# 4-bit FFN in a fused two-layer kernel: gate and up of three token units as three float32r passes over split digits

## Chip, cores and metric

The kernel runs on one core of a Trainium2 chip. Times are device microseconds of one execution; the time of the kernel before is the median of three runs, 622.34 us (621.92 to 623.31). The profile is of one further execution, 623.01 us, of which 620.9 us lie between its first and last instruction. TensorE is called PE (its weight loads PEld), VectorE DVE, ScalarE ACT, GpSimd POOL, and SP issues the DMAs.

## What is computed

Two transformer layers on 2 x 512 tokens of width 256. Each of the four steps has the form x = x + LN(f(LN(x))):

```
x = x + LN(attention(LN(x)))           # 16 heads of 128, rope, causal softmax, wo
x = x + LN(ffn_4bit(LN(x)))            # gate, up: 256 -> 2048, down: 2048 -> 256
x = x + LN(linear_attention(LN(x)))    # qkv, phi(q)*cumsum(k*v) / (phi(q)*cumsum(k)), W_out
x = x + LN(ffn_lut(LN(x)))             # 256 -> 688 -> 256, weights are 16 table values
```

The 4-bit FFN, which the change is about:

```
gate = xt @ Wg.T ; up = xt @ Wu.T      # Wg, Wu [2048, 256]: 4-bit codes times a scale per 32
inter = gelu_tanh(gate) * up
out = inter @ Wd.T                     # Wd [256, 2048]
```

## The kernel before

**Tiling.** The 1024 tokens are four units of 256 (`TU`, L41): units 0 and 1 are batch entry 0, units 2 and 3 entry 1. Attention goes head by head over an entry (32 slots, `slot`, L1149). The rest goes unit by unit. The hidden width 2048 is 16 chunks of 128 rows, `gate` and `up` are the two kinds, and the contraction of 256 is two halves (`NK`).

**PE.** Every product goes through `matmul` (L286), in float32, its 128 weight columns cut into two halves of 64 (`halved`). The profile shows each half as two records. A bank is a PSUM tile of 128 x 512; there are four tags (`mm`, `s`, `t`, `o`) of two banks each (`bank`, L243), so the third user of a tag waits until the first is read.

**4-bit FFN.** `ffn_hidden(u)` (L1089) makes two chunks at a time: four products into a `mm` bank for gate, four into an `s` bank for up, Gelu on ACT from `mm`, and the product `hT` on DVE from `s`. `ffn_out(u)` (L1117) contracts `hT` with the down weights: 32 products into an `o` bank. Its result goes to `after_ffn` (L1134): `norms` (L420) on POOL, DVE and ACT, a 32 x 32 transposition on DVE into `tr` and four DMAs that bring `tr` to `xT` (`brought`, L377), then `linear_attention` (L1340): three projections with `wqkv`, Relu and Exp on ACT, sums on POOL and DVE, running sums (`tensor_tensor_scan`) on DVE, reciprocals, products `lT` on POOL, `wout` on PE, norms again. The running sum of units 1 and 3 starts from the end of units 0 and 2. Last comes the table FFN (`silu_hidden` L1435, `silu_out` L1475).

**What sets the order.** All engines take their instructions in the order in which the program writes them. The program writes PE's work in the order of its loops, and between two pieces of it (`poll`, L262) it lets waiting chains write their next step, when a planner (`Times` L50, `Engine` L103) believes that their inputs are ready. The planner keeps a clock for each engine with a cost for each instruction; for a float32 product PE is charged 5 ns and the streams (L294). All instructions that go through the planner carry its line, L192, and all products L291. `fills` are DVE instructions without a due time, which turn table codes into weights (`select_in`, L451); they are written into gaps that the planner sees on DVE, or all at once by `flush`.

**Order around the change.** Attention of entry 1 ends together with the hidden chunks of unit 0. Then (L1323 to L1325) the attention sums are added on DVE, the remaining fills flushed, and the chain `after_attention(1)` (L1075) begins, which makes the normed and turned tokens `xT1` of units 2 and 3. The main loop (L1537 to L1543) runs, for each unit, the rest of its hidden chunks, the first bank pair of the next unit, and `ffn_out`. So the order on PE is: two banks of unit 1, out of unit 0, the rest of unit 1, two banks of unit 2, out of unit 1, and so on. `xT1` of unit 1 comes from `after_attention(0)`, during attention of entry 1.

Of the kernel before, what the change touches and what calls it, by code (L numbers as in the profile page):

```python
# [10 lines left out]
F32 = mybir.dt.float32  # L11
I32 = mybir.dt.int32
F8 = mybir.dt.float8e4
U8 = mybir.dt.uint8
# [22 lines left out]
TURNED = [P, 4, NK, HT, 32]  # L37
INTER = 688
# [7 lines left out]
AHEAD = 2.4  # L46
REST = INTER - (NO - 1) * P
# [152 lines left out]
def sandwich_kernel(  # L200
# [61 lines left out]
    def poll():  # L262
        while True:
            due = [c for c in chains if c[0] <= now[0]]
            if not due:
                return
            c = min(due, key=lambda c: c[0])
            wait = next(c[1], None)
            if wait is None:
                chains.remove(c)  # L270
            else:
                c[0] = now[0] + wait
# [23 lines left out]

    def transpose(out, in_):
        nc.tensor.transpose(out, in_, ident)  # L298
        now[0] = max(now[0], times.start("PE", [out], [in_])) + 0.11
        times.add("PE", now[0], [out], [in_])  # L300
# [14 lines left out]
    cos_sb = const.tile([P, S], F32, name="cos_sb")  # L315
    sin_sb = const.tile([P, S], F32, name="sin_sb")
    bo_sb = const.tile([P, D], F32, name="bo_sb")
# [59 lines left out]
    def brought(to, tr):  # L377
        for a in range(4):
            sync.dma_start(
                out=to[:, a].rearrange("p k j t -> p (k j t)"),  # L380
                in_=tr[32 * a : 32 * a + 32].rearrange("f c k j t -> f c (k j t)"),
            )

    def last_norms(u, y, to, eps):

        x = [xs[u][:, j, :] for j in range(HT)]

        def factors(y, eps):
            st = small.tile([P, 6], F32, tag="st", name="st")
            mv = small.tile([P, 2], F32, tag="mv", name="mv")  # L390
            vector.bn_stats(st, y)
            vector.bn_aggr(mv, st)
            ve = small.tile([P, 1], F32, tag="ve", name="ve")
            vector.tensor_scalar(ve, mv[:, 1:2], eps, None, ALU.add)
            rstd = small.tile([P, 1], F32, tag="rstd", name="rstd")
            pool.tensor_tensor(rstd, ve, mhalf[:, :1], ALU.pow)
            return mv, rstd

        first = [factors(t, eps) for t in y]
        second = []  # L400
        for j in range(HT):
            add_scaled(x[j], y[j], first[j][1])
            second.append(factors(x[j], EPS))
        yield 1.0
        n = acts.tile([P, HT, D], F32, tag="ln", name=f"n_{u}")
        tr = turning(u, 3)
        for j in range(HT):
            mv, rstd = second[j]
            vector.tensor_scalar(n[:, j, :], x[j], mv[:, 0:1], rstd, ALU.subtract, ALU.mult)
            turned_about(tr, n, j)  # L410
        brought(to, tr)
        yield 1.0
        for j in range(HT):
            mv, rstd = first[j]
            shift = small.tile([P, 1], F32, tag="shift", name="shift")
            pool.tensor_scalar(shift, mv[:, 0:1], rstd, -1.0, ALU.mult, ALU.mult)
            scalar.activation(x[j], x[j], AF.Identity, bias=shift)
        yield until(to)

    def norms(u, y, stage, to, eps=EPS, strided=False):  # L420
# [89 lines left out]
    with ExitStack() as at:  # L510
# [5 lines left out]
        dq = at.enter_context(tc.tile_pool(name="dq", bufs=1))  # L516

# [557 lines left out]
        def after_attention(b):  # L1075
            yield 0.5
            for u in (2 * b, 2 * b + 1):
                xT1[u] = late.get("lw", acts).tile(
                    TURNED, F32, tag="xT1", name=f"xT1_{u}", bufs=2
                )  # L1080

                y = [half(acc, u)[:, j, :] for j in range(HT)]
                yield from norms(u, y, 1, xT1[u], strided=True)
# [3 lines left out]
        hT1 = {}  # L1087

        def ffn_hidden(u):  # L1089
            if u % 2 == 0:  # L1090
                hT1[u] = fh.tile([P, MLP // P, TU], F32, tag="hT", name=f"hT_{u}", bufs=1)
            else:
                hT1[u] = late["lw"].tile([P, MLP // P, TU], F32, tag="hTb", name=f"hT_{u}")
            nc_u = UNIT // P
            for c2 in range(0, MLP // P, 2):
                pg, pu = bank("mm"), bank("s")
                for ps, ws in ((pg, wg_u), (pu, wu_u)):
# [15 lines left out]
                    hT1[u][:, c2 : c2 + 2, :].rearrange("p c t -> p (c t)"), ge, pu  # L1113
# [3 lines left out]
        def ffn_out(u):  # L1117
            po = bank("o")
            for t in range(HT):
                for c in range(MLP // P):  # L1120
# [3 lines left out]
                        hT1[u][:, c, t * P : (t + 1) * P],  # L1124
# [6 lines left out]
            begin(after_ffn(u, po))  # L1131
            yield

        def after_ffn(u, po):  # L1134
            xT2[u] = late["lp"].tile(TURNED, F32, tag="xT2", name=f"xT2_{u}", bufs=1)
            yield from norms(u, [po[:, j * D : (j + 1) * D] for j in range(HT)], 2, xT2[u])
# [12 lines left out]
        def slot(i):  # L1149
# [21 lines left out]
            if i == NH + 2:  # L1171
                attention_sums(0)
                begin(after_attention(0))
# [110 lines left out]
            if i == NS - 4:  # L1284
# [4 lines left out]
                    [(down_i[:, o, :], wd[:, o, :]) for o in range(NO)],  # L1289
# [34 lines left out]
        vector.flush()  # L1324
        begin(after_attention(1))  # L1325


    lw = late["lw"] = ctx.enter_context(tc.tile_pool(name="lw", bufs=1))
    lp = late["lp"] = ctx.enter_context(tc.tile_pool(name="lp", bufs=2))
    gp = ctx.enter_context(tc.tile_pool(name="gp", bufs=2))  # L1330

    ones = lw.tile([P, TU], F32, name="ones")
    pool.memset(ones, 1.0)
    wqkv_sb = lw.tile([P, NK, 3 * D], F32, name="wqkv_sb")
    sync.dma_start(out=wqkv_sb, in_=wqkv)
    wout_sb = lw.tile([P, NK, D], F32, name="wout_sb")
# [3 lines left out]
    def linear_attention(u):  # L1340
# [15 lines left out]

        def of(name, bufs=1):
            return lp.tile([P, NK, TU], F32, tag=name, name=f"{name}_{u}", bufs=bufs)
# [4 lines left out]
        for part, e, f in ((1, ek, k), (0, eq, q)):  # L1363
            ps = project(part, "mm")
            scalar.activation(flat(e), ps, AF.Relu, scale=-1.0)
            scalar.activation(flat(f), ps, AF.Relu)
            if last:

                scalar.activation(e, e, AF.Exp, scale=-1.0)
                vector.tensor_scalar(e, e, -1.0, 1.0, ALU.add, ALU.add)  # L1370
# [3 lines left out]
        ps = project(2, "s")  # L1374
        scalar.copy(flat(v), ps)
        if not last:
# [3 lines left out]
            for e, f in ((ek, k), (eq, q)):  # L1380
                vector.tensor_scalar(e, e, -1.0, 1.0, ALU.add, ALU.add)
                pool.tensor_add(f, f, e)
        yield until(k, v)
        ks, kvs, den, lT = of("ks", 2), of("kvs", 2), of("den"), of("lT")

        def running_sum(to, of_):
            for ch in range(NK):
                before = carry[to is kvs, u - 1][:, ch, TU - 1 :] if u % 2 else 0.0
# [3 lines left out]
            carry[to is kvs, u] = to  # L1392

        running_sum(ks, k)
        if not last:
            yield until(ks, q)
        vector.tensor_mul(den, q, ks)
        vector.tensor_scalar(den, den, EPS_LIN, None, ALU.add)
        vector.tensor_mul(v, k, v)
        yield until(v)  # L1400
        running_sum(kvs, v)
# [23 lines left out]
        yield from last_norms(u, y, t, 16 * EPS) if last else norms(u, y, 3, t, 16 * EPS)  # L1425
# [5 lines left out]
    hT2 = [lw.tile([P, NO, TU], F32, name=f"hT2_{j}") for j in range(2)]  # L1431
    for t in hT2:
        pool.memset(t[:, FULL, :], 0.0)

    def silu_hidden(u):  # L1435
# [12 lines left out]
        for o in range(0, NO, 2):  # L1448
# [11 lines left out]
            si = gp.tile([P, 2 * TU], F32, tag="si", name="si")  # L1460
# [76 lines left out]
    hidden = main  # L1537
    for u in range(NUNIT):
        run(hidden)
        if u + 1 < NUNIT:  # L1540
            hidden = ffn_hidden(u + 1)
            run(hidden, 2)
        run(ffn_out(u))  # L1543
    hidden = None
    vector.flush()
# [102 lines left out]
```

## Time and profile before

| what | value |
|---|---|
| median of three runs | 622.34 us (621.92 to 623.31) |
| profiled execution | 623.01 us, span 620.9 us |
| PE busy | 611.6 us, 99% of the span, 4968 records |
| PEld busy | 389.4 us, 63% |
| DVE busy | 452.0 us, 73%, 1159 instructions |
| ACT busy | 306.2 us, 49%, 716 instructions |
| POOL busy | 226.2 us, 36%, 343 instructions |
| granted PE clock | 1.00 |
| DMA | 75.61 MB, 122 GB/s over the span |

The busy shares are means over the span. Attention and what is beside it lie before 391 us, the 4-bit FFN with most of the linear attention between 391 and 550 us, the table FFN after. A PE record ends, by the profile's model, after the next one has begun, so the step from one start to the next is the time that a record costs. The same holds, to about 0.09 us, for DVE and ACT instructions that don't depend on one another. In the profile's lists a bracket at the end of a line gives the idle time of the engine ahead of the instruction and what ended it.

### The profile page before, as it was taken

What the parts mean: (1) busy time and instruction counts of PE and PEld (TensorE: products, weight loads), DVE (VectorE), ACT (ScalarE), POOL (GpSimd) and SP (SyncE); (2) the same over time, 40 slices, a digit from 0 to 9 for tenths busy, and PEclk for the clock granted to TensorE, in tenths of its full rate; (3) what the DMA queues carried; (4) which work ended last, traced back from release to release, by engine and by line L of the source; (5) the groups of instructions that cost most, each with busy time, mean ns of one, the idle gap of its engine ahead of it and who ended that gap; (6) DMA issues with size and microseconds to landing.
All of it is one profiled execution on the core that took longest, in us unless ns stands there. A gap on an engine that the chain in (4) does not pass through costs nothing.

```text
span 620.9 us, 13496 instructions
## 1 busy us (share of the span) xinstructions
PE 611.6 (99%) x4968; PEld 389.4 (63%) x4968; DVE 452.0 (73%) x1159; ACT 306.2 (49%) x716; POOL 226.2 (36%) x343
## 2 busy tenths in 40 slices
PE   9999999999999999999999999999999999999996
PEld 7555565555556546555555667777777777776665
DVE  7975788988988878877885889972472752472963
ACT  5655666576556476666656662024414223325210
POOL 5344444343243264364444300061161350162531
PEclk9999999999999999999999999999999999999999
DMA  8375867796777767787776423201001000001010
GB/s 230 108 199 147 233 183 204 194 243 179 220 216 204 194 189 199 194 233 200 193 166 156 117 63 73 77 18 35 2 7 30 2 18 18 2 1 35 18 53 18
DMA packets 53393, 75.61 MB, mean 122 GB/s; under 512 B 6992, under 2 KB 34512, under 8 KB 53328
## 3 DMA queue, kind: packets, MB, share of 16 engines
q1 hardware_dynamic: 53328, 74.76, 45.5%
q8 instruction: 39, 0.64, 0.4%
q14 instruction: 26, 0.21, 0.1%
HBM read 28.59 MB, written 1.05 MB: 48 GB/s over the span
## 4 chain that ended last, share of the span: by engine, by line
PE 95%; DMA 2%; DVE 1%; SPq 1%; ACT 0%; issue 0%; POOL 0%; DVEq 0%
PE ps_mm L291 38%; PE ps_o L291 21%; PE ps_s L291 21%; PE ps_t L291 15%; DMA pT<-turned 2%; SPq L174 1%; PE ps_o L556 1%; ACT p L192 0%; DVE rr L192 0%; DVE x L192 0%; DVE centred L192 0%; DVE p L192 0%; ACT ra L192 0%; POOL rstd L192 0%; PE ps_t L298 0%
## 5 line engine op out<-in xcount | busy, mean ns | idle before, releaser
L192 ACT ACTIVATE p<-p,mn 128x512 f32<-128x512 f32 (+3 forms) x128 | 70.4, 551 | 51.9 <-DVE mn L192 51.9
L291 PE MATMUL ps_mm<-xT,wg 128*64 128x256 f32 (+1 forms) x704 | 85.9, 379 | 0.0
L291 PE MATMUL ps_s<-xT,wu 128*64 128x256 f32 x672 | 82.0, 379 | 0.0
L291 PE MATMUL ps_t<-pT,v 128*64 128x256 f32 (+3 forms) x512 | 74.8, 433 | 2.8 <-DMA pT<-turned 2.8
L291 PE MATMUL ps_o<-wd,hT 128*64 128x256 f32 (+1 forms) x704 | 76.7, 375 | 0.0
L291 PEld LDWEIGHTS ps_mm<-xT,wg 128*64 128x64 f32 (+1 forms) x704 | 55.1, 137 | 20.5 <-ACT si L192 0.4
L291 PEld LDWEIGHTS ps_o<-wd,hT 128*64 128x64 f32 x704 | 54.7, 137 | 20.2
L192 DVE TENSOR_TENSOR hT<-ge,ps_s 128x512 f32<-128x512 f32 x32 | 21.8, 684 | 61.2 <-PE ps_s L291 36.9
L291 PEld LDWEIGHTS ps_s<-xT,wu 128*64 128x64 f32 x672 | 52.9, 137 | 19.6 <-DVE hT L192 0.3
L291 PEld LDWEIGHTS ps_t<-pT,v 128*64 128x64 f32 x512 | 39.6, 137 | 40.5 <-issue 32.3
L192 ACT ACTIVATE p<-p,rs 128x512 f32<-128x512 f32 (+3 forms) x128 | 61.1, 550 | 1.8 <-DVE rs L192 1.8
L291 PE MATMUL ps_o<-wo,oT 128*64 128x256 f32 x512 | 61.0, 379 | 0.0
L291 PE MATMUL ps_mm<-xT,wk 128*64 128x512 f32 x248 | 58.8, 592 | 0.9 <-DVE rr L192 0.9
L291 PE MATMUL ps_mm<-xT,wq 128*64 128x512 f32 (+2 forms) x256 | 59.2, 576 | 0.0
L291 PE MATMUL ps_s<-kT,qT 128*64 128x320 f32 (+5 forms) x384 | 57.4, 424 | 0.0
L291 PEld LDWEIGHTS ps_o<-wo,oT 128*64 128x64 f32 x512 | 39.4, 137 | 27.8 <-issue 14.9
L192 DVE STREAM_TRANSPOSE turned<-p 128x512 f32<-128x512 f32 (+3 forms) x128 | 53.8, 476 | 2.9 <-ACT p L192 1.6
L192 POOL TENSOR_TENSOR ra<-ra,cos_sb 128x512 f32<-128x512 f32 (+1 forms) x33 | 41.2, 1249 | 40.5 <-ACT ra L192 40.5
L192 DVE SCALAR_TENSOR_TENSOR ry<-ps_mm,cols_sb,sin_sb 128x512 f32<-128x512 f32 x54 | 40.3, 746 | 21.5 <-ACT ra L192 20.0
L291 PE MATMUL ps_mm<-wv,xTv 128*64 128x256 f32 x464 | 55.3, 379 | 0.0
L192 ACT ACTIVATE ln<-x,shift,rstd 128x256 f32<-128x256 f32 x22 | 13.3, 607 | 77.3 <-POOL shift L192 76.6
L291 PEld LDWEIGHTS ps_s<-kT,qT 128*64 128x64 f32 x384 | 35.9, 137 | 22.4 <-issue 11.6
(162 smaller groups left out, 953.6 us busy)
## 6 DMA issues: line engine op xcount, KB each, us to landing
pT<-turned SPq DMA_DIRECT2D x128, 208.0 KB, 3.9
rr<-ry SPq DMA_DIRECT2D x108, 128.0 KB, 3.0
wo<-in_wo SPq DMA_DIRECT2D x17, 256.0 KB, 4.1
wv<-in_wv SPq DMA_DIRECT2D x16, 256.0 KB, 4.0
wq<-in_wq SPq DMA_DIRECT2D x15, 256.0 KB, 4.0
wk<-in_wk SPq DMA_DIRECT2D x15, 256.0 KB, 4.9
xT<-tr SPq DMA_DIRECT2D x48, 64.0 KB, 2.1
pk_g<-in_gate_p SPq DMA_DIRECT2D x4, 256.0 KB
```

Source lines behind the costliest of these rows:

```text
L174: return write(*args, **more)
L192: return write(*args, **more)
L291: nc.tensor.matmul(out[part], lhsT=lhsT[:, part], rhs=rhs, start=start, stop=stop, **more)
L556: nc.tensor.matmul(warm[:, :P], lhsT=units, rhs=units, start=True, stop=True)
```

## The change

Gate and up of units 2 and 3, and of chunks 4 to 15 of unit 1, are no longer float32 products. Weights w and tokens x are each split in parts whose significands fit a float32r operand; three float32r products, summed in one PSUM bank, take the place of one float32 product. Pass 0 multiplies the float32r views of w and x. Pass 1 adds the product of w's low part and the tile `low` of x. Then ACT multiplies the bank in place by 1 + 1/4096, and pass 2 adds the product of the third tile of w and the tile `dif` of x. A pass is one PE instruction per half of the contraction, at the full 128 weight columns (`digits`).

- `split_tokens` makes the token parts: per 512 columns three DVE instructions and a scaling on ACT. Units 2 and 3 share one tile `xT_b`, so their products have 512 columns. Unit 1 has its own parts.
- `fetch_weights(p)` copies the weights of two chunks (a pair) by DMA, SBUF to SBUF, into the tile that holds the three parts, and `split_weights(p)` makes the other two parts: three DVE instructions of 512 columns per kind. The tiles of pairs p and p + 2 are the same. The split serves all three units.
- `ffn_hidden_of_three` writes items "e" (unit 1, 256 columns of gate and 256 of up in one `t` bank), "g" and "u" (512 columns of gate or up of units 2 and 3, in `mm` or `s`), three in flight: passes 0 and 1 and the scaling at an item's beginning, pass 2 and Gelu or the `hT` product at its end, three items later.
- New order: rest of unit 0, its `ffn_out` with the first split in between, chunks 0 to 3 of unit 1 in float32, the token splits, the joint hidden stage with the chain of unit 0 inside, then `ffn_out` of units 1, 2 and 3 in a row. Before, unit 0's chain began at the end of its `ffn_out`; now it begins with the joint stage.
- `after_attention(1)` becomes two chains, which use `last_norms` (on DVE, with POOL's power) and no longer `norms`. The fills aren't flushed before them; four of six column groups of the table FFN's down weights are made before, the other two as one piece of 512 columns after the joint stage.
- In `linear_attention` the term exp - 1 + 1 is no longer written as an instruction of its own, the copy of v is gone (the product k * v reads PSUM), the small constant is added by ACT, the projections use banks `t` and `o`, the tiles of units 1 and 3 reuse the weight tiles, and the carry is a copy of two columns.
- Constants move to other pools; the two `hT2` tiles share a buffer with `hT`; the Silu result shares `ge`.

The core of the diff (the planner's charge for a `digits` stream is 13 ns and N/2400 us):

```diff
+F32R = mybir.dt.float32r
+TOP = 0xFFFFF000 - (1 << 32)
+RADIX = 4096.0
+EARLY = 4
+EARLIER = 4
...
+    def digits(out, lhsT, rhs, first):
+        nc.tensor.matmul(out, lhsT=lhsT, rhs=rhs, start=first, stop=False, skip_group_check=True)
+        now[0] = max(now[0], times.start("PE", [out], [lhsT, rhs])) + 0.013 + math.prod(rhs.shape[1:]) / 2400
+        times.add("PE", now[0], [out], [lhsT, rhs])
...
+        def split_tokens(b):
...
+                vector.tensor_scalar(top.bitcast(I32), x.bitcast(I32), TOP, None, ALU.bitwise_and)
+                vector.scalar_tensor_tensor(dif, top, -1.0 - 1.0 / RADIX, x, ALU.mult, ALU.add)
+                yield
+                vector.scalar_tensor_tensor(low, dif.bitcast(F32), RADIX, top, ALU.mult, ALU.add)
+                scalar.mul(dif, dif.bitcast(F32), RADIX)
+                yield
...
+        def fetch_weights(p):
+            for kind in range(2):
+                w3[kind, p] = late["lb"].tile(
+                    [P, 3, NK, TU], F32R, tag=f"w3_{kind}{p % 2}", name=f"w3_{kind}_{p}"
+                )
+                sync.dma_start(out=w3[kind, p][:, 0].bitcast(F32), in_=pair_of(kind, p))
...
+        def split_weights(p):
...
+                vector.tensor_scalar(top.bitcast(I32), w.bitcast(I32), TOP, None, ALU.bitwise_and)
+                yield
+                vector.tensor_sub(w3[kind, p][:, 1], w, top)
+                yield
+                vector.scalar_tensor_tensor(
+                    w3[kind, p][:, 2], top, 1.0 + 1.0 / RADIX, w, ALU.mult, ALU.subtract
+                )
+                yield
...
+            def begun_item(n, which):
+                if which == "e":
+                    ps = bank("t")
+                    passes(ps[:, :TU], 0, n, 0, (0, 1), True)
+                    passes(ps[:, TU:], 1, n, 0, (0, 1), False)
+                else:
+                    ps = bank({"g": "mm", "u": "s"}[which])
+                    passes(ps, which == "u", n, 1, (0, 1), True)
+                scalar.mul(ps, ps, 1.0 + 1.0 / RADIX)
+                banks_of[n, which] = ps
+
+            def ended_item(n, which):
+                ps = banks_of.pop((n, which))
+                if which == "e":
+                    passes(ps[:, :TU], 0, n, 0, (2,), False)
+                    passes(ps[:, TU:], 1, n, 0, (2,), False)
+                    ge = late["gp"].tile([P, TU], F32, tag="ge1", name="ge1")
+                    scalar.activation(ge, ps[:, :TU], AF.Gelu_apprx_tanh)
+                    vector.tensor_mul(hT1[1][n], ge, ps[:, TU:])
+                    return
+                passes(ps, which == "u", n, 1, (2,), False)
+                if which == "g":
+                    ge_of[n] = fh.tile([P, S], F32, tag="ge", name="ge")
+                    scalar.activation(ge_of[n], ps, AF.Gelu_apprx_tanh)
+                else:
+                    vector.tensor_mul(both[n], ge_of.pop(n), ps)
...
+            items = [(n, w) for n in range(NC) for w in "egu" if w != "e" or n >= EARLIER]
+            for item in items + 3 * [None]:
+                if len(flight) == 3 or item is None:
+                    done = flight.popleft()
+                    ended_item(*done)
...
-    hidden = main
-    for u in range(NUNIT):
-        run(hidden)
-        if u + 1 < NUNIT:
-            hidden = ffn_hidden(u + 1)
-            run(hidden, 2)
+    fetch_weights(0)
+    fetch_weights(1)
+
+    run(main)
+    splits = split_weights(0)
...
+    turns(ffn_out(0), splits, 2)
...
+    hidden = ffn_hidden(1)
+    run(hidden, EARLIER - 2)
...
+    for _ in split_tokens(1):
+        pass
+    run(hidden, 2)
+    for _ in split_tokens(0):
+        pass
+    begin(after_ffn(0, first_po[0]))
+    slowly(ffn_hidden_of_three())
...
+    select_in(tops, [tuple(t[:, EARLY:, :].rearrange("p o d -> p (o d)") for t in (down_i, wd))])
+    for u in (1, 2, 3):
         run(ffn_out(u))
+    vector.flush()
```

## Prediction

> **What bounds the kernel now.** I read the page's engine table first, then its chain of work that ended last, then the busy time by stretch, the timeline of each engine from 390 us on, and the groups by form. The chain:
>
> ```profile
> PE 95%; DMA 2%; DVE 1%; SPq 1%; ACT 0%; issue 0%; POOL 0%; DVEq 0%
> ```
>
> TensorE is the path from end to end. By stretch (columns: length, then busy time of PE, PEld, DVE, ACT, POOL with instruction counts, granted clock, DMA share, GB/s):
>
> ```profile
> 405.00:425.00 20.00, 20.00 (x189) 14.93 (x186) 14.20 (x41) 8.74 (x17) 13.54 (x36) 1.00 0.12 27
> 425.00:474.00 49.00, 49.00 (x458) 36.59 (x456) 22.53 (x45) 15.27 (x26) 14.04 (x31) 1.00 0.08 18
> 474.00:550.00 76.00, 76.00 (x708) 56.76 (x706) 34.92 (x65) 21.87 (x35) 20.21 (x40) 1.00 0.04 8
> ```
>
> PE has no gap anywhere in the 4-bit FFN (391 to 550 us), and VectorE (DVE) is idle for half of it. So a cut in PE's streams is worth its full length, until another engine makes PE wait; the change takes from PE and gives to DVE and ScalarE (ACT). The order of instructions on each engine, listed from the two built kernels, is the same on PE up to the last `ps_o<-wo` of attention, which ends at 391.2 us. Everything to be reckoned lies behind that.
>
> **What PE saves.** The unit is one bank: four 128x128 by 256-column float32 products.
>
> ```profile
> 425.76 1.91 PE L291 MATMUL ps_mm<-xT,wg 128*64 128x256 f32 x16
> 427.49 1.91 PE L291 MATMUL ps_s<-xT,wu 128*64 128x256 f32 x16
> ```
>
> Bank follows bank after 1.727 us, so a product takes 0.432 us, made of four streams of 256 columns at 107.9 ns (106.7 ns is 256 columns at 2.4 per ns, and 1.2 ns besides). The change takes away unit 1's chunks 4 to 15 (12 x 2 kinds x 2 halves of the contraction = 48 products) and all of units 2 and 3 (128 products): 176 x 0.432 = **76.0 us**. It puts in, as listed, 16 x 2 x 3 x 2 = 192 streams of 512 columns and 12 x 2 x 3 x 2 = 144 of 256, each with its own 128-column weight load.
>
> No float32r stream stands in the trace. From below: the rows above, N/2.4 plus 1.2 ns, which gives 192 x 214.5 + 144 x 107.9 = 56.7 us. From above: the load.
>
> ```profile
> L291 PE MATMUL ps_o<-xT,wk 128*128 128x256 f32 x4 | 1.2, 380 | 0.0
> L291 PEld LDWEIGHTS ps_o<-xT,wk 128*128 128x128 f32 x4 | 0.6, 197 | 0.0
> L291 PEld LDWEIGHTS ps_mm<-xT,wg 128*64 128x64 f32 x688 | 55.0, 137 | 20.2 <-ACT si L192 0.4
> ```
>
> A 128-column float32 load took 197 ns against 137 for 64. If streams wait for it, those of 512 columns still hide it and those of 256 pay 197 ns: 192 x 214.5 + 144 x 197 = 69.6 us. (Full-width float32 itself goes at 0.44 us for two records, four streams again, so one pass at full width should be one stream.) In between is what the new helper `digits` charges in the planner, 13 ns + N/2.4: 60.7 us; its sister constant for float32, 5 ns a product, is exactly the trace's 431.7 - 426.7. I take 7 ns a stream, between the first row and this constant, nearest to the rows of the same stream: 192 x 220.3 + 144 x 113.7 = 58.7 us. Saving **17.3 us**, with 6.4 and 19.3 as ends. `wqkv`, `wout`, both down products and the last FFN keep their streams.
>
> **What DVE gets.** Durations from its own rows, spaced as they follow one another: add or multiply of 512 columns 0.60, scalar-tensor-tensor 0.66, tensor-scalar 0.34 (0.47 when the next instruction needs it), statistics with aggregate 0.55.
>
> ```profile
> 443.08 0.69 DVE L192 TENSOR_TENSOR hT<-ge,ps_s 128x512 f32<-128x512 f32 x1 [5.96 <-ACT ge L192]
> 443.68 0.42 DVE L192 TENSOR_SCALAR ek<-ek 128x512 f32<-128x512 f32 x1
> 444.02 0.42 DVE L192 TENSOR_SCALAR eq<-eq 128x512 f32<-128x512 f32 x1
> ```
>
> A pair of chunks needs 2 x (0.47 + 0.60 + 0.66) = 3.46 us of weight splits. A chunk of three units costs PE 12 x 0.220 + 12 x 0.114 = 4.0 us and DVE 1.73 + 0.60 + 0.36 = 2.7; a chunk of two units (the first four) costs PE 2.64 and DVE 2.3. The mean fits; the order on DVE's queue, at the start, does not:
>
> 1. After the attention sums (392.2) DVE does the norms of units 2 and 3. Last unit's norms in this trace, all on DVE, run from 590.17 to 596.56 with 0.8 us of other work, 5.6 us each; with the first split 11.2 + 3.5, to 406.9. They are done, DMA included, behind PE's `ffn_out(0)` (391.2 to 405.1) and four float32 banks of unit 1 (to 412.0). But DVE's next in line is the `hT` product of the first two banks, 408.8 to 409.4; behind it two halves of token splits at 0.47 + 0.78 + 0.66: 413.2. PE wants the low digits at 412.4: **0.9 us** wait.
> 2. Then on DVE: `hT` 0.6, unit 1's tokens 1.9, two steps of the second weight split 1.1, statistics 1.1, its other four steps 2.4, and only then the `hT` product that frees u0's bank (0.7): 421.0. u2 needs that bank ("s" has two). PE gets there after 24 streams: 413.3 + 5.3 = 418.6. **2.4 us.**
> 3. The up weights' low digit of the third pair comes behind the `hT` of u1 and u2 and 0.5 + 0.6 + 1.1 + 0.7 + 0.5 of other steps, at 427.7; PE is there at 425.6. **2.1 us.** After that DVE gains about 1.3 us a chunk, and unit 0's linear attention (some 7 us) fits.
>
> **What ACT gets.** 28 + 16 scalings of a bank at 0.5 us spacing: 2.4 us a chunk beside PE's 4.0. Between them stands the switch to Exp and back:
>
> ```profile
> 438.69 1.28 ACT L192 ACT_TABLE_LOAD   x1
> 439.99 0.63 ACT L192 ACTIVATE ek<-ek 128x512 f32<-128x512 f32 x1
> 440.52 0.61 ACT L192 ACTIVATE eq<-eq 128x512 f32<-128x512 f32 x1
> 441.15 1.28 ACT L192 ACT_TABLE_LOAD   x1
> ```
>
> That is 3.8 us in which no bank is scaled, where now only Gelu waits. Three banks in flight give about 2.6 us of grace before the third pass is due: **0.8 us**.
>
> **What the tail gets.** `ffn_out` of units 1, 2, 3 now stand in a row, so the chains (norms, linear attention) of units 1 to 3 have less PE work over them, and DVE's code selection for the last two column groups is spread between. Norms with their DMA need 11 to 13 us; unit 1's projection comes 11.2 us after its `ffn_out`, unit 2's 12.1, unit 1's `wout` 32.8 against 33.7 to 34.8 for its chain: **1.9 us** together. The largest is unit 3:
>
> ```profile
> 567.49 3.62 PE L291 MATMUL ps_mm<-xT,wqkv_sb 128*64 128x256 f32 x32
> 588.23 1.90 PE L291 MATMUL ps_t<-wout_sb,lT 128*64 128x256 f32 x16
> 587.36 0.46 POOL L192 TENSOR_TENSOR lT<-v,den 128x128 f32<-128x128 f32 x1 [0.35 <-DVE den L192]
> ```
>
> From its projection to its last `lT` (587.8) are 20.3 us, and PE reaches `wout` 20.7 us after the projection's start: it just fits. In the new order PE has between the two only 5.2 (projection) + 3.45 + 5.2 + 1.7 = 15.5 us. The chain loses two tensor-scalars and a copy, and gets a table switch and a transpose in its way; at 20 us PE waits **4.5 us**. Behind it PE's work and the 4.8 us after its last stream are as now.
>
> The weight fetches (256 KB each, on SP, SBUF to SBUF) wait for PE to release their buffer. The nearest row, `pT<-turned` with 208 KB, lands in 3.9 us. A pair's up buffer comes free some 5.5 us before its first use, so the cover is 1.5 us, and at the third pair the wait above hides it; a slower landing would be paid in full, at each of six pairs. Unit 0's `xT` transfers stand behind two fetches, which are free about 5 us before its data is. The other edits (constants in other pools, the running sum's carry as a copy of 0.1 us, four of six code pieces before 391 us) are off the path. I count 0 for all of these.
>
> **Sum.** The profiled execution took 623.0 us (span 620.9). 623.0 - 17.3 + 0.9 + 2.4 + 2.1 + 0.8 + 1.9 + 4.5 = 618.3; it lies 0.7 above the median of the three runs, 622.3, so I forecast **617.6 us**.
>
> **A rule that speaks against it.** In the trace the first 18 records of PE take 4.18 us, 232 ns each, and those of the same shape from 6.6 us on 0.14. The Trainium skill, TensorE: Matmul & The Clock Gate, part 1, states that an idle window of about 3.4 us drops PE to half its clock for as long. The granted clock here reads 1.00 in every stretch, because PE never idles after the start. If the 4.5 us wait met such a window, an estimate from that page is up to 1.7 us more, 619.3 us.
>
> **Rivals.**
>
> *Waits smaller than I count* (DVE's queue runs tighter, the tail's waits overlap): half of the 12.6 us of waits and the low end of the streams give 623.0 - 19.3 + 6.3 - 0.7 = 609.3. For: every wait above hangs on one place in a queue. Against: each is a sum of durations in this trace.
>
> *DVE becomes the bound of the digit stage* (the slower side). The place is its queue between `hT` of u(n), which frees a bank, and the split of the next pair: if what I found at the third pair (2.1 us) comes back at each of the five later pairs, 10.5 us are added: 628.1. It decides from 4.7 us of further waits on. For: chains of units 0 and 1 enter the same queue in order. Against: 1.3 us of slack a chunk.
>
> *Streams of 256 columns wait for loads*: 69.6 in place of 58.7 us, 628.5.
>
> *A float32r pass isn't one stream but the full-width record* (220 ns for 256 columns): 58.7 becomes 192 x 0.44 + 144 x 0.22 = 116, so 675. The change would not do what it says. The four-stream sum of float32 speaks against it.
>
> **Chances.** My forecast with its own range, 612 to 621: 0.46; the first rival 0.17; within 0.2% of 622.3 (about what a measurement of this kernel can tell from no change) 0.12; DVE's bound 0.15, the loads 0.07, full-width passes 0.03. So faster 0.63, same 0.12, slower 0.25. The range runs from 609 to 630.
>
> **What would show it.** Right: banks of six digit streams every 1.32 us; PE gaps of 1 to 2.5 us ahead of u0 to u4, released by DVE; a gap of 4 to 5 us before unit 3's `wout`, released by POOL; no change before 391 us. Wrong: digit streams above 230 ns, PE waiting on `hT` or splits all through the stage, or DVE above 90% busy there.

## The result, and the profile after

The changed kernel takes 626.56 us, the median of four runs (625.35 to 627.31), beside 622.47 us for the kernel before: a ratio of 1.0063 (95% interval 1.0042 to 1.0084). Forecast were 617.6 us and a gain. The profiled execution took 625.35 us, span 623.24, and was the shortest of the four.

The chain of work that ended last, on the page of the changed kernel:

```profile
PE 85%; DVE 6%; DMA 2%; ACT 2%; POOL 2%; issue 2%; SPq 1%; POOLq 0%; DVEq 0%; ACTq 0%
```

PE carries 85% of it and no longer 95%. The busy time by stretch, with the columns as before, shows where the rest is (the last stretch was not shown of before; PE had no gap there until its end either):

```profile
405.00:425.00 20.00, 17.01 (x102) 11.75 (x99) 15.21 (x31) 8.34 (x15) 4.12 (x9) 1.00 0.17 42
425.00:474.00 49.00, 47.43 (x282) 38.74 (x281) 29.83 (x58) 31.78 (x61) 5.00 (x5) 1.00 0.19 60
474.00:550.00 76.00, 72.84 (x628) 54.57 (x628) 49.41 (x106) 26.55 (x49) 31.05 (x66) 1.00 0.08 18
550.00:623.00 73.00, 63.15 (x600) 44.99 (x595) 43.55 (x106) 18.30 (x35) 28.75 (x63) 0.99 0.10 27
```

PE has gaps in every stretch, most of them at the start of the digit stage (3 us up to 425 us, 1.6 us behind it) and in the last stretch (5 us besides the 4.6 us that follow its last stream). DVE, at 61% between 425 and 474 us, is not full anywhere for long. The timeline of PE lists each gap (bracket: idle time and what ended it):

```profile
412.45 0.73 PE L309 MATMUL ps_mm<-x,w 128*128 128x512 f32 x2 [0.32 <-DVE x L202]
...
417.38 0.74 PE L309 MATMUL ps_mm<-x,w 128*128 128x512 f32 x2 [2.33 <-ACT ps_mm L202]
...
421.25 0.74 PE L309 MATMUL ps_s<-xT_b,w 128*128 128x512 f32 x2 [0.34 <-DVE hT_b L202]
...
428.02 0.51 PE L309 MATMUL ps_t<-x,w 128*128 128x256 f32 x2 [1.57 <-DVE w L202]
...
513.28 1.95 PE L301 MATMUL ps_t<-xT,wqkv_sb 128*64 128x256 f32 x16 [0.71 <-DMA xT<-tr]
...
534.07 1.95 PE L301 MATMUL ps_t<-xT,wqkv_sb 128*64 128x256 f32 x16 [2.44 <-ACT spare L202]
...
562.51 1.95 PE L301 MATMUL ps_o<-wout_sb,v 128*64 128x256 f32 x16 [1.46 <-DVE x L202]
...
578.72 1.08 PE L301 MATMUL ps_o<-wd,hT 128*64 128x256 f32 x8 [0.44 <-DVE hT L202]
580.93 3.70 PE L301 MATMUL ps_o<-wd,hT 128*64 128x256 f32 x32 [1.13 <-DVE hT L202]
586.44 1.08 PE L301 MATMUL ps_mm<-xT,wg 128*64 128x256 f32 x8 [1.81 <-DMA xT<-tr]
...
589.43 1.52 PE L301 MATMUL ps_t<-wout_sb,spare 128*64 128x256 f32 x12 [0.61 <-POOL spare L202]
```

4.56 us at the start of the digits, none between 428 and 513 us, 8.61 us in the tail: 13.2 us. From 428 to the stage's end at 485 us PE runs without a gap; this is its pace, on the same timeline:

```profile
430.24 0.63 PE L309 MATMUL ps_s<-xT_b,w 128*128 128x512 f32 x2
430.70 0.63 PE L309 MATMUL ps_s<-x,w 128*128 128x512 f32 x2
431.17 0.63 PE L309 MATMUL ps_t<-x,w 128*128 128x256 f32 x4
431.64 0.41 PE L309 MATMUL ps_t<-xT,w 128*128 128x256 f32 x2
```

Two streams of 512 columns take 0.467 us, 233.4 ns each; four of 256 take 0.47 to 0.48, about 120 ns each.

**The balance.** From the end of attention's last stream to PE's last stream the kernel before needs 224.8 us (391.23 to 616.05), this one 228.1 (390.52 to 618.61). Float32 streams: 704 fewer at 107.9 ns, 76.0 us out. Digit streams: 192 x 0.2334 + 144 x 0.120 = 62.1 us in. That saves 13.9 us. What is left, 3.3 + 13.9 = 17.2 us, is the 13.2 us of the brackets and 4.0 us that no bracket shows. A wait costs more than its bracket, and so does a change between float32 and float32r:

```profile
414.42 0.63 PE L309 MATMUL ps_mm<-x,w 128*128 128x512 f32 x2
417.38 0.74 PE L309 MATMUL ps_mm<-x,w 128*128 128x512 f32 x2 [2.33 <-ACT ps_mm L202]
417.95 0.63 PE L309 MATMUL ps_s<-xT_b,w 128*128 128x512 f32 x2
...
445.09 0.40 PE L309 MATMUL ps_t<-x,w 128*128 128x256 f32 x2
445.43 1.95 PE L301 MATMUL ps_o<-xT,wqkv_sb 128*64 128x256 f32 x16
447.30 0.74 PE L309 MATMUL ps_mm<-x,w 128*128 128x512 f32 x2
447.88 0.63 PE L309 MATMUL ps_mm<-xT_b,w 128*128 128x512 f32 x2
```

From 414.42 to 417.38 PE gets through two streams worth 0.47 us, so 2.49 us are lost for a bracket of 2.33, and the two streams behind the wait take 0.57 us, 0.10 too long. Steps read in this way give 0.19 to 0.27 us beside the bracket at each of the eleven waits, 2.6 us together. The 16 float32 records from 445.43 on take 1.87 us in place of 1.73, and the steps before and after them are 0.10 and 0.11 us too long: 0.14 to 0.21 us at each of eight changes of this kind, 1.4 us together.

### The profile page after: what moved, and what is told of

Same layout as the page of the kernel before. It is cut to its first block, busy times and chain, and to the rows that moved or that the text cites. A ratio compares the mean times of both kernels' runs of the same rounds, so it can differ in the third digit from the quotient of the medians.

```text
span 623.2 us, 12908 instructions
## 1 busy us (share of the span) xinstructions
PE 600.7 (96%) x4600; PEld 382.8 (61%) x4600; DVE 477.4 (77%) x1207; ACT 326.7 (52%) x762; POOL 228.1 (37%) x332
## 4 chain that ended last, share of the span: by engine, by line
PE 85%; DVE 6%; DMA 2%; ACT 2%; POOL 2%; issue 2%; SPq 1%; POOLq 0%; DVEq 0%; ACTq 0%
PE ps_mm L301 29%; PE ps_o L301 18%; PE ps_t L301 16%; PE ps_s L301 13%; PE ps_s L309 3%; PE ps_mm L309 3%; PE ps_t L309 3%; DMA pT<-turned 1%; DVE spare L202 1%; DVE x L202 1%; POOL rstd L202 1%; SPq L184 1%; DVE st L202 1%; DVE scratch L202 1%; DVE w L202 1%
## 5 line engine op out<-in xcount | busy, mean ns | idle before, releaser
L301 PE MATMUL ps_mm<-xT,wk 128*64 128x512 f32 x248 | 58.7, 592 | 0.9 <-DVE rr L202 0.9
L301 PE MATMUL ps_o<-wd,hT 128*64 128x256 f32 (+1 forms) x448 | 49.1, 374 | 1.6 <-DVE hT L202 1.6
L202 POOL TENSOR_SCALAR after<-mn 128x1 f32<-128x1 f32 x27 | 5.8, 214 | 118.9 <-DVE mn L202 107.3
L202 POOL TENSOR_TENSOR rstd<-ve,mhalf 128x1 f32<-128x1 f32 (+1 forms) x65 | 41.2, 635 | 16.4 <-DVE ve L202 11.0
L301 PE MATMUL ps_mm<-xT,wg 128*64 128x256 f32 x352 | 44.1, 379 | 1.8 <-DMA xT<-tr 1.8
L202 POOL TENSOR_SCALAR ve<-mv 128x1 f32<-128x1 f32 x43 | 12.7, 294 | 83.9 <-DVE mv L202 81.9
L202 POOL TENSOR_TENSOR qT<-ra,rr 128x512 f32<-128x512 f32 x32 | 40.9, 1279 | 5.7 <-DVE rr L202 5.7
L301 PEld LDWEIGHTS ps_o<-wd,hT 128*64 128x64 f32 x448 | 32.2, 137 | 17.5 <-DVE hT L202 2.7
L202 ACT ACTIVATE oT<-ps_t,cols_sb 128x512 f32<-128x512 f32 x32 | 22.0, 687 | 38.7 <-PE ps_t L301 38.7
```

The lines of the kernel that those rows point to most:

```text
L202: return write(*args, **more)
L301: nc.tensor.matmul(out[part], lhsT=lhsT[:, part], rhs=rhs, start=start, stop=stop, **more)
```

## The experiments

Waits are given by their brackets; ratios are to the kernel before, run beside it on the same chip.

**1. The order alone.** Float32 products stand in the joint stage again; the order, the splits and the tail stay.

```diff
                 for k in ks:
+                    if k:
+                        continue
...
-                        digits(
+                        matmul(
...
-                scalar.mul(ps, ps, 1.0 + 1.0 / RADIX)
                 banks_of[n, which] = ps
```

> The changed kernel with float32 products again in the joint stage (pass 0 as a float32 product, passes 1 and 2 and the scaling of the banks left out; the splits and fetches stay, though nothing but part 0 is read): the new order without the shorter streams. Theory A (the tail's waits come from ffn_out of units 1 to 3 standing in a row, not from the digits): no wait at the start of the joint stage, PE's tail waits as in the changed kernel (8.6 us by brackets, some 10 by step): 622 + 10 = 632, up to 634 with lost clock. Rival B (the tail's waits come from the digit stage being short, so that the chains of units 0 and 1 are late): waits in the tail under 3 us, 622 to 625.

Measured: 636.06 us, 1.0247 (1.0227 to 1.0267). PE's timeline has one gap of 1.21 us in the joint stage, and 9.66 us in the tail. The largest of them, and one of the five from 571 to 599 us that are those of the changed kernel from 562 to 590 us, to 0.01 us:

```profile
523.39 2.82 PE L301 MATMUL ps_t<-xT,wqkv_sb 128*64 128x256 f32 x16 [4.20 <-DMA xT<-tr]
...
571.65 1.95 PE L301 MATMUL ps_o<-wout_sb,v 128*64 128x256 f32 x16 [1.46 <-DVE x L202]
```

Theory A held for the tail; it had not foreseen the gap of 1.21 us in the joint stage, and the time is 2 us above its range. Without one float32r stream the new order costs 14.6 us. By PE's balance it is 13.7: 10.9 of waits, 1.7 of lost clock (experiment 9), and 1.1 that is left for the restarts after seven gaps. The tail's waits come from the order, with the tail's other edits, and not from the digits. The digits, put on top of it, take 10.4 us away by the same balance (238.5 to 228.1).

**2 to 4. The start of the digit stage.** Three edits, each of which moves something in a queue. In 2 the split of unit 1's tokens comes later:

```diff
-    for _ in split_tokens(0):
-        pass
     begin(after_ffn(0, first_po[0]))
...
+                    if item == (EARLIER - 2, "u"):
+                        for _ in split_tokens(0):
+                            pass
```

> The split of unit 1's tokens (three DVE instructions, one ACT scaling) is written behind the second chunk's items instead of ahead of the first digit stream. Theory A (each wait hangs on its place in a queue): the waits of PE before u0's end (417.4, 2.5 us by step) and at 421.3 (0.5) go, the one at 428 (1.6 to 1.8, for the split weights) stays or grows by at most the 1.9 us of DVE that now stand ahead of it; net 1 to 3 us less than the changed kernel, 623.5 to 625.5. Rival B (DVE has a fixed amount to do before the third pair of chunks, so the wait only moves): the wait at 428 grows to 4.5 us and the time stays at 626 to 627.

Measured: 626.62 us, 1.0074 (1.0062 to 1.0086), no gain. What made PE wait at 417.4 in the changed kernel is seen on its ACT timeline:

```profile
416.09 0.63 ACT L202 ACTIVATE x<-x 128x512 fp32r<-128x512 f32 x1 [2.54 <-DVE x L202]
416.74 0.58 ACT L202 ACTIVATE ps_mm<-ps_mm 128x512 f32<-128x512 f32 x1
```

The scaling of unit 1's token part waits for DVE and holds up the first scaling of a bank, which waits for nothing else. In the run that gap is gone, and PE's timeline shows others:

```profile
412.73 0.73 PE L309 MATMUL ps_mm<-x,w 128*128 128x512 f32 x2 [0.33 <-DVE x L202]
...
419.61 0.74 PE L309 MATMUL ps_s<-xT_b,w 128*128 128x512 f32 x2 [1.01 <-DVE hT_b L202]
...
423.05 0.73 PE L309 MATMUL ps_s<-xT_b,w 128*128 128x512 f32 x2 [0.36 <-DVE hT_b L202]
...
427.30 0.51 PE L309 MATMUL ps_t<-x,w 128*128 128x256 f32 x2 [1.86 <-DVE w L202]
```

The gap before u2 (1.01, DVE's `hT_b`) had been hidden behind ACT's. The sum falls by 1.0 us only, and the profiled run lost 1.7 us of clock. In time rival B is nearer, but the wait of 4.5 us that it named did not come (1.86).

In 3 the split of the second weight pair is written ahead of unit 1's float32 banks, where DVE was idle (the loop that writes the rest of the token chains moves ahead of these banks with it):

```diff
-            splits = split_weights(1)
+            splits = iter(())
...
-    hidden = ffn_hidden(1)
-    run(hidden, EARLIER - 2)
     while any(c[1] in last_turns for c in chains):
         now[0] = max(now[0], min(c[0] for c in chains))
         poll()
+    for _ in split_weights(1):
+        pass
+    hidden = ffn_hidden(1)
+    run(hidden, EARLIER - 2)
```

> The changed kernel with the weight split of the second pair (six DVE instructions, 3.5 us) written ahead of unit 1's first bank, into DVE's idle time from 405 to 412, in place of the first items. Theory A (order on DVE, not its amount of work, makes PE wait at the start): the waits at 421.3 and 428 go; the one at 417.4 (2.3), which hangs on ACT's scaling of unit 1's tokens, stays: 2.2 us less than the changed kernel, about 624.3. Rival B (DVE is the bound there in sum): they come back one or two pairs later, as in the run that moved the token split: 626 to 627.

Measured: 627.32 us, 1.0098 (1.0082 to 1.0113), no gain. The gap at 421 is gone, the first low digit waits 1.18 us, since its tokens are now split behind the weights, and the gap before the third pair stays to the hundredth. DVE's and PE's timelines around it:

```profile
424.74 0.69 DVE L202 TENSOR_TENSOR hT_b<-ge,ps_s 128x512 f32<-128x512 f32 x1 [1.04 <-PE ps_s L309]
425.35 0.42 DVE L202 TENSOR_SCALAR top<-wg 128x512 int32<-128x512 int32 x1
...
429.00 0.68 DVE L202 TENSOR_TENSOR w<-wu,top 128x512 fp32r<-128x512 f32 x1
```

```profile
429.73 0.51 PE L309 MATMUL ps_t<-x,w 128*128 128x256 f32 x2 [1.57 <-DVE w L202]
```

So it is neither DVE's work in sum nor its backlog: DVE had idled 1.04 us. The third pair uses the tiles of the first, and its split is written only behind u1's end. From there DVE goes through `hT_b`, three steps of the gate split, 1.1 us of unit 0's norms, `hT_b` again, and two steps for up, 429.7; PE, with chunks of two units, is there at 428.0.

In 4 chunk 4 begins with the 512-column items, so that unit 1's item is wanted later:

```diff
-            items = [(n, w) for n in range(NC) for w in "egu" if w != "e" or n >= EARLIER]
+            items = [(n, w) for n in range(NC) for w in ("gue" if n == EARLIER else "egu") if w != "e" or n >= EARLIER]
...
-                    if n % 2 == 0 and which == ("e" if n >= EARLIER else "g") and n:
+                    if n % 2 == 0 and which == ("e" if n > EARLIER else "g") and n:
```

> The changed kernel with the first chunk of three units (chunk 4) begun by the 512-column items of units 2 and 3 and unit 1's item last, so that the third pair's up weights are wanted 1 us or more later. Theory C (the wait at 428 is a chain: the tile of pair 0 comes free with the last pass of its up item, then 0.6 us of issue, 1.9 us to land, two DVE instructions, and two-unit chunks give it only 5.6 us): the wait falls from 1.6 to 0.3 to 0.9, whatever stands in DVE's queue. Rival D (DVE's queue): it stays at 1.6. The chain of unit 0 is written at other places by this, so the tail may shift by a few us either way and the total tells little.

Measured: 625.35 us, 1.0054 (1.0038 to 1.0070). The gap falls from 1.57 to 0.30, with 0.59 further on:

```profile
428.22 0.73 PE L309 MATMUL ps_s<-xT_b,w 128*128 128x512 f32 x2 [0.30 <-DVE hT_b L202]
436.30 0.51 PE L309 MATMUL ps_t<-xT,w 128*128 128x256 f32 x2 [0.59 <-DVE hT L202]
```

The number fits theory C, but its chain was told wrongly: the split reads the original weights, not the fetched copy. The copies land at 425.78 and 427.16 in experiment 3, while DVE gets to up only at 428.06. By these timelines, what counts is where the split is written (behind u1, with which the tile comes free) and what stands before it in DVE's queue. That is step 3 of the prediction; it is read from the timelines and has no run of its own.

**5. Code selection in one block.**

```diff
     select_in(tops, [tuple(t[:, EARLY:, :].rearrange("p o d -> p (o d)") for t in (down_i, wd))])
+    vector.flush()
     for u in (1, 2, 3):
```

> The code selection of the last two column groups (some 20 DVE instructions, 11 us) is written in one block before the output products of units 1 to 3, instead of into gaps up to 524 us. Theory A: unit 2's norms start at once, its turned tokens land some 4 us sooner, so the wait ahead of unit 2's projection (534.1, 2.6 us by step) goes and that ahead of unit 1's projection (513.3, 0.9) as well: 3.5 us less than the changed kernel, about 623. Rival B: what is won comes back at unit 3's chain (568 to 590 us): 626.

Measured: 625.63 us, 1.0060 (1.0048 to 1.0072). Both gaps named are gone. In the changed kernel this had been DVE's timeline ahead of unit 2's norms:

```profile
519.58 0.43 DVE L202 BATCH_NORM_STATS2 st<-ps_o 128x6 f32<-128x256 f32 x1 [8.58 <-PE ps_o L301]
...
520.15 0.72 DVE L202 COPY_PREDICATED scratch<-scratch,scratch 128x512 int32<-128x512 int32 x1
520.91 1.01 DVE L202 TENSOR_SCALAR scratch<-scratch,differ,lut_sb 128x512 int32<-128x512 int32 x2
521.95 1.54 DVE L202 COPY_PREDICATED scratch<-scratch,scratch 128x512 int32<-128x512 int32 x2
523.52 0.74 DVE L202 COPY_PREDICATED wd<-scratch,scratch 128x512 int32<-128x512 int32 x1
524.16 0.41 DVE L202 BATCH_NORM_STATS2 st<-ps_o 128x6 f32<-128x256 f32 x1
```

Four microseconds of table codes stand between the two statistics of one unit, so its tokens come 4 us late. The releaser that the profile names at 534.07, ACT's `spare`, ended at 533.98, but it writes nothing that this product reads; the last transfer of `xT` landed at 533.93, and with the block the gap is gone. But with the block the planner writes unit 0's `wout` later (at 490.8 in the changed kernel, between products of unit 1), where its o bank is still being read:

```profile
504.97 1.95 PE L301 MATMUL ps_o<-wout_sb,v 128*64 128x256 f32 x16 [1.93 <-DVE x L202]
```

3.15 us of gaps out (and the 0.34 at 421), 1.93 in, and the knot at 577 to 590 us as it was: the time is rival B's, the place where it came back is another.

**6. Unit 2's norms on DVE, its `wout` in a t bank.**

```diff
-        po = bank("t" if last else "o")
+        po = bank("t" if u >= 2 else "o")
...
-        yield from last_norms(u, y, t, 16 * EPS, 3) if last else norms(u, y, t, 16 * EPS, 3)
+        yield from last_norms(u, y, t, 16 * EPS, 3) if u >= 2 else norms(u, y, t, 16 * EPS, 3)
```

> Unit 2's product with wout goes to a t bank in place of an o bank, and the norms behind it are those on DVE (with POOL's power) in place of those that scale on ACT. Theory A: the wait for the o bank (562.5, 1.7 us) goes; unit 2's norm no longer stands behind Exp and the table loads of unit 3 on ACT, its tokens land some 8 us sooner, four more bank pairs of unit 2 come between unit 3's projection and its wout, and the waits at 578.7, 580.9, 586.4 and 589.4 (together 4.9) shrink to under 1.5: 5 us less than the changed kernel, about 621.5. Rival B: unit 3's chain from its projection to its last lT (21.6 us here) is what PE waits for; taking the waits ahead of it away makes the one before its wout grow to 4 us: 1.7 less, about 625.

In the changed kernel ACT and DVE had done this ahead of the gaps from 578.7 us on:

```profile
571.64 1.28 ACT L202 ACT_TABLE_LOAD   x1
...
574.95 1.08 ACT L202 ACTIVATE ln<-x,shift,rstd 128x256 f32<-128x256 f32 x2
...
577.34 1.12 ACT L202 ACTIVATE si<-ps_mm 128x512 f32<-128x512 f32 x3
```

```profile
577.97 0.69 DVE L202 TENSOR_TENSOR hT<-si,ps_s 128x512 f32<-128x512 f32 x1 [8.17 <-ACT si L202]
```

Unit 1's `si` and `hT`, and unit 2's norm (`ln`), stand on ACT behind the Relu, Exp and table loads of unit 3's chain.

Measured: 624.97 us, 1.0050 (1.0030 to 1.0070). All five gaps from 562 to 590 (5.45 us) are gone, with unit 3's `wout` waiting for nothing; 0.61, 1.67 and 1.07 us came in their place at 575, 602 and 606: at 602 unit 3's own norms stand ahead of unit 2's last `hT` on DVE, and at 606 PE waits for unit 3's tokens to land. So 2.1 us were won of the 5 expected. The two edits were not run one by one. The time is rival B's, but unit 3's chain from projection to `lT`, its reason, was not what PE waited for.

**7. How a stream reads its tokens.**

```diff
-                            chunk(x3[b][k], kc),
+                            x3[b][k].rearrange("p a k j t -> p (a k j t)")[:, kc * (S if b else TU) : (kc + 1) * (S if b else TU)],
```

(`S` is 512 and `TU` 256; `b` is 1 for units 2 and 3, 0 for unit 1.)

> The digit streams read 512 (unit 1: 256) neighbouring elements of the token tiles in place of runs of 32 (other tokens than they should; same counts and sizes). If the runs of 32 are what makes a float32r stream 233.4 ns instead of 213.3 (and 120.7 instead of 106.7), the steps fall to about 214.5 and 108, and the stage is 5 to 6 us shorter; if it is a cost of every float32r instruction, the steps stay at 233 and 121.

Measured, in one run of 627.64 us: two streams of 512 columns take 0.454 us, 227 ns each; those of 256 about 118 ns. The total says little, since both of its gaps above 2 us were followed by lost clock (experiment 9). A float32 stream of 256 columns takes 107.9 ns, and one of 512, in experiment 1, 214.6 (eight records in 1.72 us), though it reads the same tile in the same runs of 32. So the runs explain 6 of the 19 ns by which a float32r stream of 512 columns is longer and 2 of the 12 at 256, and in float32 they cost nothing that shows. The other 10 to 12 ns belong to every float32r stream here. What they are was not found. The loads are not waited for: they take 186 to 193 ns, and streams of 256 columns follow one another in about 120.

**8. All edits together, in three steps.** First those of 2, 5 and 6, with six float32 chunks:

```diff
-EARLIER = 4
+EARLIER = 6
```

> All three edits together, and six chunks of unit 1 in float32 instead of four before the joint stage (which costs PE 0.6 us: two chunks at 1.73 instead of 1.45). Theory A: of the 15.4 us of PE's waits (5.3 at the start of the digits, 10.1 in the tail) 2 to 3 are left, and with PE never idle for long the clock reads 1.000 in every run, which takes away the 1 to 1.5 us that the changed kernel's other runs have over its profiled one: 612 to 614. Rival B (the waits move on; DVE's and unit 3's chains bound): 620 to 625.

Measured: 621.32 us, 0.9994 (0.9983 to 1.0005); gaps of 3.0 and 5.3 us, rival B's size. Then four float32 chunks again, the early split of 3, and two edits more:

```diff
-        po = bank("t" if u >= 2 else "o")
+        po = bank("o" if u == 1 else "t")
...
-            run(hidden, 4)
+            run(hidden, 99 if u == 1 else 4)
```

> Early weight split, later split of unit 1's tokens, code selection in one block, unit 2's norms on DVE, wout of units 0, 2 and 3 in t banks, and all of unit 2's hidden banks of the table FFN ahead of unit 1's output product, so that after unit 3's wout 9.5 us of PE work are left to cover its norms. Four float32 chunks of unit 1 as in the changed kernel. Theory A: 13.2 us of waits (brackets) fall to about 3, no wait over 2 us is left, so no clock is lost: PE's 224.8 us behind attention in the kernel before become 224.8 - 13.8 + 4 = 215, the time 612 to 613. Rival B (each wait taken away comes back elsewhere): 618 to 621.

Measured: 619.12 us, 0.9968 (0.9955 to 0.9981), faster than before, but still rival B's size: 6.7 us of gaps, one of 3.00 us among them, where unit 2's output product waits for an o bank that is read behind unit 3's norms. At last that bank was changed and only half of the weight split written early:

```diff
+    second = split_weights(1)
+    for _ in range(3):
+        next(second)
     hidden = ffn_hidden(1)
...
-                po[t, cs.start] = bank("t" if cs.start else "o")[:, :D]
+                tag = ("t", "mm")[t] if u == 2 else "t" if cs.start else "o"
+                po[t, cs.start] = bank(tag)[:, :D]
```

> The best version so far (early weight split, later split of unit 1's tokens, code selection in one block, unit 2's norms on DVE, unit 2's table banks ahead of unit 1's output product) with two waits of it taken away: only the gate half of the second weight split is early, so that the token split starts 1.7 us sooner (1.2 us of wait at the first low digit), and unit 2's last product goes to a t and an mm bank, so that it needn't wait for unit 1's result to be read from the o banks (3.0 us, with 3.4 us of lost clock in the profiled run). Theory A: waits of 2.5 to 3 us in all, clock 1.000 at all times: 613 to 615. Rival B (they come back): 617 to 619.

Measured: **615.31 us, 0.9904 (0.9887 to 0.9922)**, faster than both kernels, and theory A's size to 0.3 us. All of PE's gaps behind attention:

```profile
413.19 0.73 PE L309 MATMUL ps_mm<-x,w 128*128 128x512 f32 x2 [0.33 <-DVE x L202]
426.21 0.51 PE L309 MATMUL ps_t<-x,w 128*128 128x256 f32 x2 [1.85 <-DVE w L202]
...
565.75 1.95 PE L301 MATMUL ps_t<-xT,wqkv_sb 128*64 128x256 f32 x16 [0.61 <-ACT spare L202]
593.86 1.08 PE L301 MATMUL ps_mm<-xT,wg 128*64 128x256 f32 x8 [0.96 <-DMA xT<-tr]
```

3.75 us instead of 13.2, and PE needs 217.5 us behind attention: 224.8 - 13.9 + 3.75 leaves 2.9 for restarts and changes. The saving of the streams was there all along; the kernel before had no gap behind attention, so there PE had nothing to win by the edits of the tail alone.

**9. The clock**, read from all profiles. The profiled run of experiment 6 has two gaps above 2 us, 2.32 ending at 419.2 and 2.41 ending at 536.9. Stretches behind them (granted clock is the third column from the end):

```profile
420.00:424.00 4.00, 4.00 (x12) 3.10 (x11) 3.90 (x9) 1.57 (x4) 2.82 (x5) 0.58 0.01 4
...
536.00:540.00 4.00, 3.15 (x16) 2.09 (x18) 4.00 (x6) 0.72 (x1) 2.29 (x4) 0.58 0.05 13
```

In each, 4 x 0.42 = 1.7 us were lost: half the clock for 3.4 us, which begins during the gap or up to 1.5 us after it. Of the 13 gaps of 2.3 us and more in these profiles, 9 were followed by it; none of 1.93 us and less was. The 3.00 us gap of the second step of 8 cost twice that. In the changed kernel's profiled execution neither gap (2.33, 2.44) was hit, its mean clock 0.999; its other three runs have 0.996 to 0.997, which fits one such loss each (1.7 of 624 is 0.003), and they lie 0.8 to 2.0 us above it. In the runs of experiment 6 the clock reads 1.000 twice (623.42 and 623.77 us) and 0.995 to 0.997 four times (624.53 to 628.04). The profile of the last version, with no gap above 1.85, reads 1.000; one of its five runs has 0.996 all the same and is 1.8 us longer than their median, and what cost it that is not recorded.

## Why the prediction was wrong

- **What bounds, and nothing before 391 us:** right. PE is the path, and attention ended 0.7 us from where it had.
- **PE's saving, 17.3 us:** 76.0 out was right. The step "I take 7 ns a stream" was mis-sized: over the N/2.4 of that sum it was 20 ns at 512 columns and 13 at 256, so 62.1 us in place of 58.7 and a saving of 13.9. The planner's constant (13 ns) was nearer than the row of float32 streams that I preferred. This is 3.4 us of the miss, and "digit streams above 230 ns", which I had named as a sign of being wrong, came (233.4).
- **Restarts and changes, not in the sum:** I priced each wait by its idle time and the change between float32 and float32r at nothing, without a reason. They are 2.6 and 1.4 us.
- **0.9 for the first digits:** 0.32 (0.6 with the restart). The place was right, the size too large.
- **2.4 before u2:** the size came (2.33 + 0.34), at another place, so it was luck. I had followed DVE's queue and not ACT's: ACT's scaling of unit 1's tokens held up the first bank scalings at 417.4. Behind it the wait that I meant was 0.34, and 1.01 once ACT's was taken away.
- **2.1 before the third pair:** 1.57, for the reason given, and it doesn't come back at later pairs, as forecast.
- **0.8 for the table switch in the digit stage:** none; the tables are loaded at 456.0 and 459.4 us, and PE has no gap there.
- **1.9 for the chains of units 1 and 2 and unit 1's `wout`:** the wait that was most too small. There were 0.71, 2.44 and 1.46 us. I had named the code selection between the norms, and then priced only the missing PE work; the o bank that unit 2's `wout` shares with the table FFN's result I had not looked up.
- **4.5 before unit 3's `wout`:** 3.99, right in size and stretch, but spread over four gaps of which only the last (0.61) hangs on unit 3's `lT`, so the size was luck too. The others hang on ACT and DVE queues in which unit 3's chain stands ahead of unit 1's `hT` and unit 2's tokens; experiment 6, in which they go, supports it.
- **No clock in the sum:** the median lies 1.2 us above the profiled run, which fits the clock of the other three runs. I had named it, for one wait of 4.5 us, and its size, 1.7 us, is what one loss costs. My reason for the clock of 1.00 before, that PE never idles, was not quite so: that trace has four gaps of 0.7 to 1.1 us between 49 and 233 us, and lost nothing by them; and its first 18 records begin 0.22 us apart, not 0.23. The Trainium skill, TensorE: Matmul & The Clock Gate, part 1, gives half a clock for about 3.4 us, which the runs here confirm, after an idle window as long, which they don't: gaps of 2.3 us were enough.
- **Sum.** Profile to profile, 618.3 was forecast and 625.35 came: 3.4 from the streams, 4.0 from restarts and changes, 0.6 from the waits (13.2 for 12.6), less 0.9 won ahead of 391 us and behind the last stream. From profile to median I took 0.7 off, and 1.2 had to be added: 1.9. Together 9.0 us.
- **The rivals:** "DVE becomes the bound", 628.1, came near the time but not the cause: DVE was at 61%, nothing waited from the fourth pair on. Streams that wait for loads, and full-width passes, are refuted by 120 and 233.4 ns.

So the steps that failed are the 7 ns a stream (20 and 13: 3.4 us), the restarts and changes put at nothing (4.0 us) and the clock left out (1.9 us with the step from profile to median). The waits themselves came to nearly what I had added up, 13.2 for 12.6, though by luck: those of the first digits, the third pair, the table switch and unit 3 were too large, that of units 1 and 2 was too small, and two hung mostly on other queues than I said. As a whole, a saving of 17 us was set against a reordering put at 12.6. Experiment 1 puts the reordering alone at 14.6, and the streams, on top of it, give back less than that (10.4 us).

## What to carry to other kernels

Price a new order by itself: keep the old operations, run the new order, and the difference of the traces tells what must be won elsewhere. Where PE was gapless, follow every queue that the new instructions enter (ACT's as well as DVE's) and every bank and tile that a moved product shares; a wait taken away can uncover the next. The edits of 2, 5 and 6 took 1.0, 1.6 and 2.5 us out of the sum of PE's gaps alone, and 4.9 together (with six float32 chunks). In time they gave next to nothing alone (1.0074, 1.0060 and 1.0050, beside 1.0063 for the changed kernel) and paid only together (0.9994), when no gap above 1.93 us was left and the clock read 0.998 or more in every run. And a gap of PE above 2 us can cost more than its length: experiment 9 has 1.7 us on top of it in 8 of 13 cases, and 3.4 us in one.

## What the runs showed of the hardware

- A float32r stream of 256 columns with a 128-column weight load repeats every 120 ns, though its load takes 188 ns; one of 512 every 233.4 (227 with consecutive tokens). A float32 stream takes 107.9 ns for 256 columns and 214.6 for 512.
- A wait of PE costs 0.19 to 0.27 us beside the bracket that the profile gives for it, a change between float32 and float32r products 0.14 to 0.21 us.
- Half the granted clock for 3.4 us at 9 of 13 gaps of 2.3 us or more (for 6.8 us at the one of 3.00), at none of 1.93 or less.
- DVE writes float32r at the pace of float32: 0.69 us for 512 columns in both.
